# A two-layer image kernel: weights of the final sum on both partition halves, tokens kept by partition, VectorE in the last strips' attention

## The chip, the core and the metric

The kernel runs on one core of a Trainium2 chip. Its engines work side by side, each in the order of its own instruction queue: TensorE (PE) multiplies matrices into PSUM, VectorE (DVE) and ScalarE (ACT) work on SBUF and PSUM, GpSimd (POOL) works on SBUF, and SyncE (SP) issues DMAs. ScalarE issues DMAs too; all of them run on the core's 16 DMA engines. The metric is the device time of one execution in microseconds (us); lower is better.

## What is computed

The input x has 16 images of 64 x 64 pixels and 128 channels, all in f32. First a group norm and a 3x3 convolution give each channel of each pixel an offset, and x is sampled at the moved place by bilinear interpolation. Then comes an attention in which each token attends among the 16 entries of each of its own 8 heads, and at last a mixture of 64 experts, in which each expert takes the 8 tokens of an image that score highest for it.

```python
x = x + deformable_sample(group_norm(x))            # conv gives the offsets
t = to_tokens(x)                                    # 16 images, 4096 tokens, 128 channels
qkv = layer_norm(t) @ w_qkv + b_qkv                 # per head of 16 channels:
attn = softmax((q * C ** -0.5)[..., :, None] * k[..., None, :])
t = t + einsum('bhlij,bhlj->bhli', attn, v) @ w_proj + b_proj

n = layer_norm(t)
probs = softmax(n @ gate_w.T + gate_b, over tokens)
vals, idx = top_k(probs, 8)                         # per image and expert
pooled = sum over the 8 of vals * n[idx]            # one vector per image and expert
h = gelu([pooled, 1] @ weight1[expert])
out_e = [h, 1] @ weight2[expert]                    # 16 images x 64 experts x 128
t[idx] += vals * out_e                              # back to the chosen tokens
```

The kernel writes the last line as a dense sum: for each image a matrix of weights (64 experts x 4096 tokens, zero where a token wasn't chosen) times the experts' outputs (64 x 128), added to t.

## The kernel before

**Two stages.** `Images` works through the 16 images; `finish` then computes all experts and the final sum. Between the two stand a few tensors in device memory: `t2_d`, the tokens after attention (16 x 2 MB), `wt_d`, the weights of the final sum (16 x 1 MB), and `oe_d`, the experts' outputs.

**The image stage.** An image is cut into 8 strips of 512 pixels (`NCH`, `CHW`), a strip into 4 token tiles of 128 (`NA`). `image()` gathers the instructions of all parts of an image in a `Work` list: the convolution of the next strip, the sampling (`sample`), the attention of the strips behind it (`tokens`), the choice of tokens of the image before (`tail`), and the preparation of the next one (`prep`). Each instruction has a slot. `Work.order()` then simulates the engines with estimated durations and sorts the instructions by when they would be ready (80 ns per slot of haste); the hand-made order is emitted as it comes out. [...] Image 0 and image 15 are emitted by themselves; images 1 to 14 are one loop whose body is emitted once. The instructions of the image stage are all recorded by one helper and stand under line 190 in the profile.

**The attention of a strip** (`tokens`) runs through 8 groups, two per token tile, with four heads each (`group(i)`). For each group: `score` (two instructions of 128 x 1024 on GpSimd: q times k, minus the largest value), `expo` (exponential on ScalarE, sum `den` on VectorE), `weigh` (one more on GpSimd into `ev`, sum `att` on VectorE). The score tiles `sc` are two, used in turn; `ev` is one. At the end `second` adds the projection to the tokens `t1` and stores them to `t2_d`, in two DMAs of 64 partitions each: `strip` puts pixel rows and columns where they belong in the image, and partition 2r+h holds half h of the strip's part of image row r. In the last image nothing follows, so the attention of its last strips runs on by itself once the sampling is over.

**The last stage** (`finish`). Experts are taken in fours: `weights` loads them on SP's queue (three buffers), `layers` computes them (PSUM tiles `hps`, `tps`, `yps2`, two buffers each) and stores the outputs to `oe_d` from ScalarE's queue. The inner function `tokens` (line 1350) loads what the final sum needs of an image: `wt`, 64 partitions of 16 KB, and `t2c`, 128 partitions, by two DMAs in pieces of 2 KB. It has four buffers (`cmb`); four images are loaded early, among the experts. `add` (line 1358) loads the image's expert outputs `oe` on ScalarE's queue and then, for each of 8 strips, multiplies four times (a weight tile of 64 experts x 128 tokens is the stationary operand, `oe` of 64 x 128 the moving one) into one PSUM bank (`cops`, two buffers), adds the bank to the tokens on VectorE, and at the end stores the image in two DMAs from ScalarE's queue. An f32 matmul is two instructions on TensorE, so an image has 64.

The order of `finish` is not made by hand: the framework schedules it and places the waits. On ScalarE's queue it comes out as three loads of oe, then six stores, then the next three loads, and so on.

Of the kernel before, what the change touches and what calls it, by code (L numbers as in the profile page):

```python
# [19 lines left out]
P = 128  # L20
B, IMG, C = 16, 64, 128
NPIX = IMG * IMG
NCH = 8
# [39 lines left out]
@with_exitstack  # L63
def conv_attn_moe_kernel(
    ctx: ExitStack,
    tc: tile.TileContext,
    x: bass.AP,
    conv_w: bass.AP,
    conv_b: bass.AP,
    w_qkv: bass.AP,  # L70
    b_qkv: bass.AP,
    w_proj: bass.AP,
    b_proj: bass.AP,
    gate_w: bass.AP,
    gate_b: bass.AP,
    weight1: bass.AP,
    weight2: bass.AP,
    out: bass.AP,
):
    nc = tc.nc  # L80

    dram = ctx.enter_context(tc.tile_pool(name="dram", bufs=1, space=DRAM))
    t2_d = dram.tile([B, NPIX, C], F32, name="t2_d")
    wt_d = dram.tile([B, E, NPIX], F32, name="wt_d")
    oe_d = dram.tile([B, E, C], F32, name="oe_d")

    const = ctx.enter_context(tc.tile_pool(name="const", bufs=1))
    pooled = const.tile([P, E, B], F32, name="pooled")

    with ExitStack() as s:  # L90
        Images(s, tc, x, conv_w, conv_b, w_qkv, b_qkv, w_proj, b_proj, gate_w, gate_b,
               dram, t2_d, wt_d, pooled).run()
    with ExitStack() as s:
        finish(s, tc, weight1, weight2, pooled, t2_d, wt_d, oe_d, out)
# [232 lines left out]
class Images:  # L327
# [583 lines left out]

    def tokens(self, b, k, slot, dense=False):
        plan = Work(self.nc, self.tc)
# [7 lines left out]

        def copy(ap, t, load):
            for h in range(2):
                at, rows = strip(ap)[:, h], t.rearrange("(r h) a c -> r h (a c)", h=2)[:, h]
                nc.sync.dma_start(*((rows, at) if load else (at, rows)))

# [3 lines left out]
        xres, t1 = self.xres[k % 2], self.t1[k % 2]  # L930
        add(-6, lambda: copy(self.x, xres, True))
        add(0, lambda: nc.scalar.activation(
# [60 lines left out]
        def group(i):  # L993
# [3 lines left out]
                ap[:, nh * i : nh * (i + 1)] for ap in (top, den, att)]  # L997

        def score(i):
            sc, (qs, ks, _), (ts, _, _) = group(i)  # L1000
            nc.gpsimd.tensor_tensor(sc, bcast(qs, 3, HD), bcast(ks, 2, HD), ALU.mult)
            nc.gpsimd.tensor_tensor(sc, sc, bcast(ts, 3, HD), ALU.subtract)

# [6 lines left out]
        def weigh(i):  # L1010
            sc, (_, _, vs), (_, _, at) = group(i)
            nc.gpsimd.tensor_tensor(self.ev, sc, bcast(vs, 2, HD), ALU.mult)
            plan.slot += 2
            nc.vector.tensor_reduce(at, self.ev, AX.X, ALU.add)
# [32 lines left out]
        def second():  # L1047
            v = t1.rearrange("p a c -> p (a c)")
            nc.vector.tensor_tensor(v, self.bank, v, ALU.add)
            copy(self.t2_d, t1, False)  # L1050

# [105 lines left out]
    def image(self, b, before, following):  # L1157
# [25 lines left out]
        for k in range(NCH):  # L1183
            work.take(self.tokens(b, k, STEPS * (k + 1) + 6), 0, end, 0)
            if k + 1 < NCH:
                work.take(self.conv(k + 1, STEPS * k), 0, SLOTS, 0)
# [95 lines left out]
def finish(ctx, tc, weight1, weight2, pooled, t2_d, wt_d, oe_d, out):  # L1282
# [8 lines left out]
    hp = ctx.enter_context(tc.tile_pool(name="exph", bufs=2))  # L1291
    lp = ctx.enter_context(tc.tile_pool(name="cmb", bufs=4))
    pp = ctx.enter_context(tc.tile_pool(name="finp", bufs=2, space=PSUM))
    nf, rows = FF // P, 32
    ident = one.tile([P, P], F32, name="ident2")
# [22 lines left out]
    def layers(e0, w1, b1, w2, b2):  # L1318
# [7 lines left out]
        nc.scalar.activation(h, hps, AF.Gelu)  # L1326
        tps = pp.tile([P, nf, P], F32, name="tps")
        for n in range(nf):
            nc.tensor.transpose(tps[:, n, :], h[:, P * n : P * (n + 1)], ident)  # L1329
        hT = hp.tile([P, nf, P], F32, name="hT")  # L1330
        nc.vector.tensor_copy(hT, tps)  # L1331
        yps = pp.tile([P, C], F32, name="yps2")
        nc.tensor.matmul(yps, chosen, b2, start=True, stop=False)
# [13 lines left out]
    def rows_of(t):  # L1347
        return t.rearrange("(r h) q a c -> r h q (a c)", h=2)

    def tokens(b):  # L1350
        wt = lp.tile([E, NPIX], F32, name="wt")
        nc.sync.dma_start(wt, wt_d[b])
        t2 = lp.tile([P, NCH, NA, C], F32, name="t2c")
        for h in range(2):
            nc.sync.dma_start(rows_of(t2)[:, h], strips(t2_d[b])[:, h])
        return wt, t2

    def add(b, wt, t2):
        oe = hp.tile([E, C], F32, name="oe")
        nc.scalar.dma_start(oe, oe_d[b])  # L1360
        for k in range(NCH):
            ops = pp.tile([P, NA, C], F32, name="cops")
            for a in range(NA):
                nc.tensor.matmul(ops[:, a, :], wt[:, CHW * k + a : CHW * (k + 1) : NA], oe,  # L1364
                                 start=True, stop=True)
            nc.vector.tensor_tensor(t2[:, k], t2[:, k], ops, ALU.add)  # L1366
# [40 lines left out]
```

## Time and profile before

| | us |
|---|---|
| median of 3 runs (9387.57 to 9394.68) | 9387.69 |
| the profiled execution | 9384.91 |
| its span in the trace | 9383.1 |
| image stage and choice of tokens, to about | 8880 |
| experts, from the first weight DMA to the last, SP's queue | 8879.8 to 9053.9 |
| final sum, from the first load of oe to the end | 9066.2 to 9383.1 |
| a repeated image (13 distances between 14 stores of weights, 822.2 to 7877.8) | 542.7 |

Busy times over the whole span: PE 8515.6, VectorE 7196.0, ScalarE 6572.7, GpSimd 7619.6 us. The costliest groups that bear on the change are these (count; busy us in all; mean ns of one): `ev<-sc,qkv` on GpSimd 1024; 2429.6; 2373, `sc<-qkv` 1024; 1987.7; 1941, `sc<-sc,top` 1024; 1988.5; 1943, and on VectorE `den<-sc` 1024; 1239.7; 1211 and `att<-ev` 1024; 1235.4; 1206. In the final sum VectorE's `t2c<-t2c,cops` comes 128 times with 687 ns at the median, always within 2 ns of it.

How to read it: a window's busy time tells which engine had no room there; the chain of waits tells what the end waited for; the queues' shares tell how much of the 16 DMA engines' time a stage used. A share over the whole span mixes the stages, so it is read stage by stage below. The program's names stand without their numbers: `t2c` is the token tile of the final sum, and `t` in the image stage is `t1`; `t2_d` shows as `t_d`.

### The profile page before, as it was taken

How to read it: one execution, taken by the hardware profiler on the slowest of the kernel's cores; microseconds unless marked ns; L12 is line 12 of the kernel's file. 1: busy time of each engine (PE TensorE's matmuls, PEld its weight loads, DVE VectorE, ACT ScalarE, POOL GpSimd, SP SyncE). 2: the span in 40 equal slices, each digit the busy share in tenths (PEclk: the TensorE clock that was granted, in tenths of full speed). 3: DMA queues.
4: the chain of work that ended last, by engine and by line, in shares of the span. 5: the costliest groups of instructions: out<-in, count | busy, mean ns of one | idle time of the engine just before them, and what ended most of it. 6: DMA issues, size and time to landing. Idle time of an engine off the chain costs nothing. (4 is left out here: it accounts for less than half of the span.)

```text
span 9383.1 us, 373512 instructions
## 1 busy us (share of the span) xinstructions
PE 8515.6 (91%) x158305; PEld 4589.8 (49%) x159622; DVE 7196.0 (77%) x10154; ACT 6572.7 (70%) x8082; POOL 7619.6 (81%) x5698
## 2 busy tenths in 40 slices
PE   8999999899999989999998999999999999999467
PEld 4545445454544545454454545445454544444247
DVE  4788787878878887887888788888878788788412
ACT  4777777777777777777777777777777777777300
POOL 2898888889888888988888898988889889889500
PEclk9999999999999999999999999999999999999655
DMA  6666666666676666667666666666666676666277
GB/s 161 178 178 175 178 176 181 175 186 177 178 182 174 182 173 185 179 176 183 173 182 172 183 182 177 182 172 183 172 181 182 177 184 172 179 177 174 77 232 239
DMA packets 1327871, 1672.08 MB, mean 178 GB/s; under 512 B 443680, under 2 KB 660512, under 8 KB 1324128
## 3 DMA queue, kind: packets, MB, share of 16 engines
q1 hardware_dynamic: 1305952, 1613.25, 63.7%
q10 hardware_dynamic: 20224, 34.61, 1.0%
q8 instruction: 1262, 20.68, 1.0%
q14 instruction: 433, 3.55, 0.1%
HBM read 1378.16 MB, written 268.96 MB: 176 GB/s over the span
## 5 line engine op out<-in xcount | busy, mean ns | idle before, releaser
L190 DVE SCALAR_TENSOR_TENSOR prod<-chat,yps 128x1024 f32<-128x1024 f32 x2048 | 2472.2, 1210 | 672.0 <-PE yps L190 214.1
L190 ACT ACTIVATE rhat<-yps 128x1024 f32<-128x1024 f32 x2048 | 2079.9, 1021 | 1112.9 <-PE yps L190 412.1
L190 POOL TENSOR_TENSOR ev<-sc,qkv 128x1024 f32<-128x1024 f32 x1024 | 2429.6, 2373 | 278.5 <-ACT sc L190 232.4
L190 PE MATMUL yps<-rhat,xr 32*32 32x176 f32 (+1 forms) x131072 | 2468.7, 275 | 117.9 <-ACT rhat L190 113.2
L190 PE MATMUL cbank<-pad,wconv 128*128 128x512 f32 x4608 | 2530.3, 636 | 38.4 <-DVE far L190 9.5
L190 PEld LDWEIGHTS yps<-rhat,xr 32*32 32x32 f32 x131072 | 1809.3, 104 | 1199.8 <-ACT rhat L190 451.4
L190 POOL TENSOR_TENSOR sc<-qkv 128x1024 f32<-128x1024 f32 x1024 | 1987.7, 1941 | 81.8 <-POOLq L1202 47.5
L190 POOL TENSOR_TENSOR sc<-sc,top 128x1024 f32<-128x1024 f32 x1024 | 1988.5, 1943 | 45.2 <-ACT top L190 36.4
L190 DVE TENSOR_REDUCE den<-sc 128x64 f32<-128x1024 f32 x1024 | 1239.7, 1211 | 256.7 <-ACT sc L190 256.3
L190 DVE TENSOR_REDUCE att<-ev 128x64 f32<-128x1024 f32 x1024 | 1235.4, 1206 | 259.9 <-POOL ev L190 215.9
L190 ACT ACTIVATE sc<-sc 128x1024 f32<-128x1024 f32 x1024 | 1078.8, 1053 | 447.9 <-POOL sc L190 408.8
L190 ACT ACTIVATE chat<-chat,cbi,csc 128x1024 f32<-128x1024 f32 x1024 | 1260.0, 1235 | 36.3 <-DMA chat<-cc_d 35.7
L190 PE MATMUL yps<-parts,sel 128*128 128x512 bf16 x2779 | 950.6, 385 | 291.7 <-DVE prod L190 255.9
L190 ACT ACTIVATE chat<-chat,cbi 128x1024 f32<-128x1024 f32 x1024 | 1162.5, 1143 | 56.1 <-DMA chat<-cc_d 50.8
L190 PE MATMUL acc<-prod,red 128*32 128x512 f32 x8192 | 1116.2, 613 | 85.9 <-issue 5.3
L190 PEld LDWEIGHTS cbank<-pad,wconv 128*128 128x128 f32 x4608 | 741.9, 190 | 902.8 <-issue 769.1
L190 PEld LDWEIGHTS <-sel 128*128 128x128 bf16 x4096 | 355.2, 98 | 1124.5 <-issue 1074.7
L190 DVE RECIPROCAL den<-den 128x128 f32<-128x128 f32 x512 | 479.9, 937 | 4.3
L190 PE MATMUL bank<-wqkv,tr 128*128 128x384 f32 x1024 | 419.5, 505 | 17.5 <-DVE qkv L190 11.1
L190 PEld LDWEIGHTS acc<-prod,red 128*32 128x32 f32 x8192 | 164.2, 108 | 446.3 <-issue 438.0
L190 DVE SCALAR_TENSOR_TENSOR qkv<-bank,rstd,bqkv 128x384 f32<-128x384 f32 x512 | 309.4, 604 | 93.2 <-PE bank L190 92.8
L190 DVE SCALAR_TENSOR_TENSOR cd<-cbank,cb,iot 128x256 f32<-128x256 f32 x512 | 229.1, 474 | 185.4 <-PE cbank L190 185.3
(162 smaller groups left out, 8124.2 us busy)
## 6 DMA issues: line engine op xcount, KB each, us to landing
chat<-cc_d SPq DMA_DIRECT2D x8192, 128.0 KB
xr<-xn_d SPq DMA_DIRECT2D x512, 128.0 KB
pc_d<-pc SPq DMA_DIRECT2D x128, 384.0 KB
parts<-pc_d SPq DMA_DIRECT2D x768, 64.0 KB
xl<-in_x_dram SPq DMA_DIRECT2D x128, 256.0 KB
xres<-in_x_dram SPq DMA_DIRECT2D x256, 128.0 KB
xn_d<-wt SPq DMA_DIRECT2D x128, 256.0 KB
cc_d<-cd SPq DMA_DIRECT2D x128, 256.0 KB
```

What stands on the lines that cost most here:

```text
L190: getattr(engine, fn)(*args, **kwargs)
```

## The change

It has three parts.

1. In the final sum the 4096 columns of weights of an image are put on both halves of the partitions: experts for the first 2048 tokens on partitions 0 to 63, for the last 2048 on 64 to 127, by two DMAs. `oe` is loaded twice, once on each half. Strips k and k + 4 are then multiplied in turn, the one from the lower 64 rows of the array and the other from the upper 64, into two PSUM banks. `cops` gets four banks in a pool of its own; `tps` and `yps2` go down to one bank each. The `cmb` pool has five buffers instead of four, and five images are loaded early, after every third group of experts, instead of four.
2. `t2_d` holds the tokens as they lie in SBUF: per image and partition, all 8 strips one behind the other (16 KB). A strip is stored by one DMA of 128 rows of 2 KB instead of two, and an image is loaded by one DMA with 16 KB per partition instead of two with 2 KB pieces.
3. In the last image, `engine(i)` gives `score` and `weigh` of some groups to VectorE: of strip 6 the groups 4 and 7, of strip 7 the groups 1, 4 and 7. In all other strips `alone` is 8 and no group moves.

```diff
--- before.py
+++ after.py
@@ -80,7 +80,7 @@
     nc = tc.nc
 
     dram = ctx.enter_context(tc.tile_pool(name="dram", bufs=1, space=DRAM))
-    t2_d = dram.tile([B, NPIX, C], F32, name="t2_d")
+    t2_d = dram.tile([B, P, NCH, NA * C], F32, name="t2_d")
     wt_d = dram.tile([B, E, NPIX], F32, name="wt_d")
     oe_d = dram.tile([B, E, C], F32, name="oe_d")
 
@@ -909,7 +909,8 @@
 
 
 
-    def tokens(self, b, k, slot, dense=False):
+
+    def tokens(self, b, k, slot, dense=False, alone=HEADS):
         plan = Work(self.nc, self.tc)
         nc = plan
 
@@ -919,16 +920,16 @@
                 v = v.rearrange("b r w c -> b (r w) c")
             return v.rearrange("b (r q h a) c -> (b q) r h (a c)", r=IMG, q=NCH, h=2)[k]
 
-        def copy(ap, t, load):
+        def load(ap, t):
             for h in range(2):
-                at, rows = strip(ap)[:, h], t.rearrange("(r h) a c -> r h (a c)", h=2)[:, h]
-                nc.sync.dma_start(*((rows, at) if load else (at, rows)))
+                nc.sync.dma_start(
+                    t.rearrange("(r h) a c -> r h (a c)", h=2)[:, h], strip(ap)[:, h])
 
         def add(rel, fn):
             plan.add(slot + rel, fn)
 
         xres, t1 = self.xres[k % 2], self.t1[k % 2]
-        add(-6, lambda: copy(self.x, xres, True))
+        add(-6, lambda: load(self.x, xres))
         add(0, lambda: nc.scalar.activation(
             self.tr[0], self.acc, AF.Identity, bias=0.0 if dense else self.norm[:, 0:1],
             scale=1.0 if dense else self.norm[:, 1:2]))
@@ -996,10 +997,13 @@
             return self.sc[i % 2], [heads(s, a)[:, hs] for s in range(3)], [
                 ap[:, nh * i : nh * (i + 1)] for ap in (top, den, att)]
 
+        def engine(i):
+            return nc.vector if i >= alone and i % 3 == 1 else nc.gpsimd
+
         def score(i):
             sc, (qs, ks, _), (ts, _, _) = group(i)
-            nc.gpsimd.tensor_tensor(sc, bcast(qs, 3, HD), bcast(ks, 2, HD), ALU.mult)
-            nc.gpsimd.tensor_tensor(sc, sc, bcast(ts, 3, HD), ALU.subtract)
+            engine(i).tensor_tensor(sc, bcast(qs, 3, HD), bcast(ks, 2, HD), ALU.mult)
+            engine(i).tensor_tensor(sc, sc, bcast(ts, 3, HD), ALU.subtract)
 
         def expo(i):
             sc, _, (_, ds, _) = group(i)
@@ -1009,7 +1013,7 @@
 
         def weigh(i):
             sc, (_, _, vs), (_, _, at) = group(i)
-            nc.gpsimd.tensor_tensor(self.ev, sc, bcast(vs, 2, HD), ALU.mult)
+            engine(i).tensor_tensor(self.ev, sc, bcast(vs, 2, HD), ALU.mult)
             plan.slot += 2
             nc.vector.tensor_reduce(at, self.ev, AX.X, ALU.add)
 
@@ -1047,7 +1051,9 @@
         def second():
             v = t1.rearrange("p a c -> p (a c)")
             nc.vector.tensor_tensor(v, self.bank, v, ALU.add)
-            copy(self.t2_d, t1, False)
+            nc.sync.dma_start(
+                at_image(self.t2_d, b).rearrange("b p k f -> (b p) k f")[:, k],
+                t1.rearrange("p a c -> p (a c)"))
 
         plan.together(slot + rel + 5.5, proj)
         add(rel + 6, second)
@@ -1181,7 +1187,8 @@
             for t in range(4, 8):
                 work.add(4 * t - 14, lambda: self.load_rows(work, t))
         for k in range(NCH):
-            work.take(self.tokens(b, k, STEPS * (k + 1) + 6), 0, end, 0)
+            alone = HEADS if following or k < 6 else 4 * (7 - k)
+            work.take(self.tokens(b, k, STEPS * (k + 1) + 6, alone=alone), 0, end, 0)
             if k + 1 < NCH:
                 work.take(self.conv(k + 1, STEPS * k), 0, SLOTS, 0)
         work.add(SLOTS - STEPS - 8, lambda: self.reach(work))
@@ -1289,8 +1296,10 @@
     one = ctx.enter_context(tc.tile_pool(name="finc", bufs=1))
     wp = ctx.enter_context(tc.tile_pool(name="expw", bufs=3))
     hp = ctx.enter_context(tc.tile_pool(name="exph", bufs=2))
-    lp = ctx.enter_context(tc.tile_pool(name="cmb", bufs=4))
+    lp = ctx.enter_context(tc.tile_pool(name="cmb", bufs=5))
     pp = ctx.enter_context(tc.tile_pool(name="finp", bufs=2, space=PSUM))
+    p1 = ctx.enter_context(tc.tile_pool(name="finp1", bufs=1, space=PSUM))
+    cpp = ctx.enter_context(tc.tile_pool(name="cmbp", bufs=4, space=PSUM))
     nf, rows = FF // P, 32
     ident = one.tile([P, P], F32, name="ident2")
     make_identity(nc, ident)
@@ -1324,12 +1333,12 @@
                              start=False, stop=True)
         h = hp.tile([P, FF], F32, name="h")
         nc.scalar.activation(h, hps, AF.Gelu)
-        tps = pp.tile([P, nf, P], F32, name="tps")
+        tps = p1.tile([P, nf, P], F32, name="tps")
         for n in range(nf):
             nc.tensor.transpose(tps[:, n, :], h[:, P * n : P * (n + 1)], ident)
         hT = hp.tile([P, nf, P], F32, name="hT")
         nc.vector.tensor_copy(hT, tps)
-        yps = pp.tile([P, C], F32, name="yps2")
+        yps = p1.tile([P, C], F32, name="yps2")
         nc.tensor.matmul(yps, chosen, b2, start=True, stop=False)
         for n in range(nf):
             for e in range(EG):
@@ -1347,23 +1356,31 @@
     def rows_of(t):
         return t.rearrange("(r h) q a c -> r h q (a c)", h=2)
 
+
+
     def tokens(b):
-        wt = lp.tile([E, NPIX], F32, name="wt")
-        nc.sync.dma_start(wt, wt_d[b])
+        wt = lp.tile([P, NPIX // 2], F32, name="wt")
+        for h in range(2):
+            nc.sync.dma_start(wt[E * h : E * (h + 1)], wt_d[b][:, NPIX // 2 * h :][:, : NPIX // 2])
         t2 = lp.tile([P, NCH, NA, C], F32, name="t2c")
+        nc.sync.dma_start(t2.rearrange("p k a c -> p k (a c)"), t2_d[b])
+        return wt, t2
+
+    def add(b, wt, t2):
+        oe = hp.tile([P, C], F32, name="oe")
         for h in range(2):
-            nc.sync.dma_start(rows_of(t2)[:, h], strips(t2_d[b])[:, h])
-        return wt, t2
-
-    def add(b, wt, t2):
-        oe = hp.tile([E, C], F32, name="oe")
-        nc.scalar.dma_start(oe, oe_d[b])
-        for k in range(NCH):
-            ops = pp.tile([P, NA, C], F32, name="cops")
+            nc.scalar.dma_start(oe[E * h : E * (h + 1)], oe_d[b])
+        for k in range(NCH // 2):
+            ops = [cpp.tile([P, NA, C], F32, name="cops") for _ in range(2)]
             for a in range(NA):
-                nc.tensor.matmul(ops[:, a, :], wt[:, CHW * k + a : CHW * (k + 1) : NA], oe,
-                                 start=True, stop=True)
-            nc.vector.tensor_tensor(t2[:, k], t2[:, k], ops, ALU.add)
+                for h in range(2):
+                    es = slice(E * h, E * (h + 1))
+                    nc.tensor.matmul(
+                        ops[h][:, a, :], wt[es, CHW * k + a : CHW * (k + 1) : NA], oe[es],
+                        start=True, stop=True)
+            for h in range(2):
+                at = k + NCH // 2 * h
+                nc.vector.tensor_tensor(t2[:, at], t2[:, at], ops[h], ALU.add)
         for h in range(2):
             nc.scalar.dma_start(
                 strips(out[b].rearrange("r w c -> (r w) c"))[:, h], rows_of(t2)[:, h])
@@ -1371,7 +1388,7 @@
     early = []
     for i, e0 in enumerate(range(0, E, EG)):
         layers(e0, *weights(e0))
-        if i % 4 == 2:
+        if i % 3 == 2:
             early.append(tokens(len(early)))
     for b in range(B):
         add(b, *(early[b] if b < len(early) else tokens(b)))
```

More of the change, by code (lines that the diff above doesn't have):

```diff
@@ L1350, in tokens @@
     def tokens(b):
-        wt = lp.tile([E, NPIX], F32, name="wt")
-        nc.sync.dma_start(wt, wt_d[b])
+        wt = lp.tile([P, NPIX // 2], F32, name="wt")
+        for h in range(2):
+            nc.sync.dma_start(wt[E * h : E * (h + 1)], wt_d[b][:, NPIX // 2 * h :][:, : NPIX // 2])
         t2 = lp.tile([P, NCH, NA, C], F32, name="t2c")
-        for h in range(2):
-            nc.sync.dma_start(rows_of(t2)[:, h], strips(t2_d[b])[:, h])
+        nc.sync.dma_start(t2.rearrange("p k a c -> p k (a c)"), t2_d[b])
         return wt, t2
     def add(b, wt, t2):
-        oe = hp.tile([E, C], F32, name="oe")
-        nc.scalar.dma_start(oe, oe_d[b])
-        for k in range(NCH):
-            ops = pp.tile([P, NA, C], F32, name="cops")
-            for a in range(NA):
-                nc.tensor.matmul(ops[:, a, :], wt[:, CHW * k + a : CHW * (k + 1) : NA], oe,
-                                 start=True, stop=True)
-            nc.vector.tensor_tensor(t2[:, k], t2[:, k], ops, ALU.add)
+        oe = hp.tile([P, C], F32, name="oe")
[3 more added lines that the diff above has]
+            ops = [cpp.tile([P, NA, C], F32, name="cops") for _ in range(2)]
+            for a in range(NA):
+                for h in range(2):
[3 more added lines that the diff above has]
+                        start=True, stop=True)
+            for h in range(2):
+                at = k + NCH // 2 * h
+                nc.vector.tensor_tensor(t2[:, at], t2[:, at], ops[h], ALU.add)
         for h in range(2):
```

## The prediction, written before the result was known

> **What bounds the kernel now.** I first read the busy time by stretch (the columns after the window and its length: PE, weight load, VectorE, ScalarE, GpSimd, each in us, then clock, DMA share, GB/s), because a share over 9383 us hides the stages.
>
> ```profile
> 8500.00:8550.00 50.00, 49.35 (x1007) 24.05 (x1014) 40.47 (x57) 38.40 (x45) 46.88 (x36) 1.00 0.62 173
> 8700.00:8750.00 50.00, 26.57 (x467) 13.54 (x471) 35.24 (x55) 23.26 (x31) 48.84 (x37) 0.76 0.17 49
> 8750.00:8800.00 50.00, 10.34 (x27) 5.55 (x27) 25.44 (x36) 11.97 (x18) 49.32 (x38) 0.53 0.03 11
> 9150.00:9200.00 50.00, 39.43 (x170) 39.16 (x169) 14.35 (x22) 0.00 (x0) 0.00 (x0) 0.50 0.92 295
> 9300.00:9350.00 50.00, 44.62 (x191) 44.66 (x192) 15.85 (x23) 0.00 (x0) 0.00 (x0) 0.50 0.62 202
> ```
>
> Three regimes: the image pipeline, where PE and GpSimd are both full; the last image's end (8700 to about 8815), where GpSimd alone is full and VectorE half idle; and the final sum after 9066, where PE and DMA share the load. The chain of waits (start, us, what) shows how they share it:
>
> ```profile
> 9066.16 1.99 DMA oe<-oe_d
> 9068.18 45.18 PE cops L1364 x192
> 9113.38 0.70 DVE t2c L1366
> ...
> 9115.79 16.50 DMA oe<-oe_d
> 9132.42 45.15 PE cops L1364 x192
> ...
> 9305.38 45.15 PE cops L1364 x192
> 9350.55 0.70 DVE t2c L1366
> 9351.25 7.47 issue
> 9358.72 15.29 PE cops L1364 x64
> ```
>
> Images go in threes: 192 matmuls in 45.15 us (235 ns each, 64 per image, so 15.05 us per image), then PE stands until the next oe has landed behind the stores. These stops are 19.1, 10.6, 13.1, 13.9 and 8.2 us, mean 13.0. So 241 of 317 us are PE and the rest is waiting. The DMA queues of 9066 to 9384 (packets, MB, share of 16 engines):
>
> ```profile
> q1 hardware_dynamic: 13632, 37.75, 40.0%
> q10 hardware_dynamic: 18176, 34.08, 29.8%
> ```
>
> Together 70% of 318 us, 222 us. Stores (q10): 94.8 us for 16 images, 5.9 each. For the loads I cut windows in which one kind is alone on q1: weights wt in 9085 to 9098, then tokens t2c in 9135 to 9147.
>
> ```profile
> q1 hardware_dynamic: 80, 1.05, 36.2%
> q1 hardware_dynamic: 1197, 2.35, 53.1%
> ```
>
> wt: 36.2% of 13 us is 4.7 us for 1.05 MB, 223 GB/s. t2c: 53.1% of 12 us is 6.4 us for 2.35 MB, 369 GB/s, 5.7 us per image of 2.1 MB.
>
> [...]
> - [...] Here no two 64-row tiles run at once; but the 32x32 tiles of yps do: 64 matmuls in 1.23 us in the timeline, with 275 ns for one.
> - [...]
> - [...] in one-element sums that differ only in where an input lies:
>
> ```profile
> L190 DVE TENSOR_TENSOR gmv<-gmv 128x1 f32<-128x1 f32 x32 | 23.4, 731 | 1.1
> L190 DVE SCALAR_TENSOR_TENSOR gmv<-bank,gmv 128x1 f32<-128x1 f32 x16 | 2.4, 152 | 0.5 <-PE bank L190 0.5
> ```
>
> - [...]
>
> **The change part by part**, against the profiled execution: 9384.9 us, span 9383.1 and 1.8 around it. The median of the runs is 2.8 above it.
>
> *PE in the final sum.* 64 matmuls per image stay, but neighbours lie in the two row halves: 32 x 235 ns = 7.5 us per image, 120 in all. Bounds: 15.05 (no overlap) and 7.5; I take 7.5 because of yps. VectorE needs 8 x 0.69 = 5.5 us per image and is not next; the four cops banks let PE fill two while two are drained.
>
> *DMA in the final sum: what is late next.* wt comes in two half DMAs; I take 4.7 us as before[...] (bounds 2.9, its bytes at 369 GB/s, and 4.7). t2c comes as 128 packets of 16 KB in one DMA instead of 1024 of 2 KB in two; nearest row 5.7[...]; I take 5.4. From above: 9.4, if [...] the 16 KB packets, which wt has too, made its 223 GB/s. Stores stay at 5.9. Three images now cost PE 22.5 + 13.0 of stop = 35.5 us and DMA 3 x (4.7 + 5.4 + 5.9) = 48 us; at the best share seen in 50 us, 0.92, that is 52. So DMA sets the pace. 11 images are loaded in the stage (five beforehand instead of four): 11/3 x 52 = 191. The other five stores: 5 x 5.9 / 0.92 = 32. Start: oe 2, PE of one image 7.5, first store's way 2, so 12. End: last sum to last byte, 8 as before (9375 to 9383). Sum 243 against 317: **-74**. Bounds: no gap in the DMA (176 + 29.5 + 20 = 226, -91) and a share of 0.70 as now (206 / 0.70 + 2 = 296, -21). The second oe DMA costs ScalarE's queue about 0.6 us an image, in front of the waiting matmuls; DMA as the pace covers it; without that cover five stops grow by 3 us in all. On SP one DMA more for wt and one fewer for t2c cancel.
>
> *Expert layers (8880 to 9066).* A fifth image is loaded between the weights on SP, before the last ones: 4.7 + 5.4 = 10.1 us of DMA where the share is mostly 0.8 to 0.9, less 4 x 0.3: **+10**. Bounds 0 (it fits the gaps) and +13. One buffer for tps and yps2 costs nothing: the next group's 3.9 us of hps matmuls stand between a tps and its 0.70 us copy; exposed it would be 16 x 1 us.
>
> *Last strips' attention.* A group costs GpSimd 1.93 + 1.93 + 2.34 = 6.2 us. Strip 6 gives away groups 4 and 7, strip 7 groups 1, 4, 7: 31 us off GpSimd. On VectorE no such instruction is in the trace; nearest is prod, equal in shape, 1.21 us: 3.6 per group. [...] 5 x (6.2 - 3.6) = 13 net. VectorE, in order, waits with each of 15 instructions for a GpSimd one of about 2 us; behind it stand the den and att reductions that free sc and ev, which GpSimd needs. VectorE goes from 25 to some 42 busy of 50 us; I give back 3: **-10**. Bounds: -31 [...] and +5 (reductions late). The tail of logits and pooling (8815 to 8880) only shifts.
>
> *Tokens by partition in the loop.* One t2_d store per strip instead of two: SP loses an issue of 0.54 us, 8 per image, same bytes, same 2 KB packets. It isn't on the chain: **0**. But the planner sorts all instructions by simulated readiness, so one sync item fewer can shift the order of everything in 16 images. I take ±16 us (0.2% of 14 x 543 us, the length of a repeated image).
>
> Sum: -74 + 10 - 10 + 0 = -74: 9311 for such an execution, **9314** as a median.
>
> **Rivals.**
> - *Long packets (0.12).* t2c at 9.4 us: three images 60 us, /0.92 = 65; 11/3 x 65 + 32 + 20 = 290, -27; layers +10 + 5 x 3.7 = +28; attention -10: -9, 9379. For: wt is the only load with such packets and the slow one. [...]
> - *No overlap in the array (0.05).* 15.05 us per image stay: 241 + 65 of stops + 3 = 309, -8; with +10 and -10 it is 9380. For: clock 0.50 and weight loads (39.16 of 39.43 us) fill the time; they could be served singly. Against: yps.
> - *A better pack (0.10).* No gaps and wt at 2.9: 226 - 11 x 1.8 = 206, -111; attention -31; layers +5: -137, 9251. For: sums for which 0.92 was reached. [...]
> - *The loop's new order is worse (0.08): slower.* In the 14 repeated images PE and GpSimd are both at 94% or more, SP issues loads in the planner's order, and a product waits where its column is late. It decides from 74 / 14 = 5.3 us (1.0%) per image; at 7.5 us it is +105 - 74 = +31: 9419. Against: the removed issue only unloads SP.
>
> **How the numbers follow.** Forecast 0.65: 9314, own range 9280 to 9350. Faster by over 0.2% (19 us, about what a measurement here can tell from no change) is below 9369: the forecast, the better pack and a third of the long packets (layers' gaps), 0.65 + 0.10 + 0.04 = 0.79, plus 0.05 of the two PE/DMA rivals helped by the loop: 0.84. Same 0.08. Slower 0.08. Range 9272 to 9375: it leaves out 0.08 slower, half of the better pack and a part of the rivals near 9380.
>
> **What would show it.** Right: three images' cops in 22 to 25 us; a DMA share over 0.85 from about 20 us into the sum until the loads end; t2c packets of 16 KB at 5 to 6 us per image; GpSimd's last ev about 10 us earlier; the loop at 543 us per image. Wrong: cops at 15 us per image; DMA idle while PE waits for oe (then order and not bandwidth bounds, and the sum stays near 296); GpSimd no earlier in spite of 15 instructions fewer; a loop length changed by more than 1 us per image.

## The result and the profile after

The changed kernel takes 9292.88 us (median of 4 runs, 9286.93 to 9295.11) against 9389.76 us for the kernel before (4 runs, 9387.57 to 9394.68): a ratio of 0.9895, 95% interval 0.9878 to 0.9912. The profiled execution takes 9292.38 us with a span of 9290.6, 92.5 us less than that of before.

To see where they went I cut both spans at the same marks: the first and the last of the 14 stores of weights in the loop (13 repeated images lie between), SP's first load of expert weights, the issue of the first oe, the end. "Last image" is what lies between the last loop store and the first expert load, "layers" from there to oe. All in us, one profiled execution each; the lower rows belong to the experiments below. The loop of after stands unchanged in e1, e3 and e4 and takes 541.4 to 541.6 us there, so 0.7 us per repeated image, 8 us in all, is within the spread of single executions; the final sum of after stands unchanged in e3, e9 and e12 and takes 245.2 to 246.0.

| kernel | first store | repeated image | last image | layers | final sum | median of runs |
|---|---|---|---|---|---|---|
| before | 822.2 | 542.74 | 1002.0 | 186.4 | 316.9 | 9389.76 |
| after | 817.9 | 542.08 | 986.9 | 192.9 | 245.9 | 9292.88 |
| e1, halves in turn | 815.2 | 541.62 | 989.9 | 192.9 | 322.6 | 9364.25 |
| e2, tokens by image | 823.6 | 542.73 | 991.4 | 198.5 | 231.8 | 9302.33 |
| e3, GpSimd alone | 815.1 | 541.41 | 999.4 | 194.5 | 246.0 | 9304.13 |
| e4, oe at once | 816.1 | 541.64 | 989.1 | 194.2 | 204.0 | 9245.47 |
| e5, wt in one load | 815.4 | 541.6 | 989.8 | 181.5 | 237.5 | 9273.81 |
| e6, e4 and e5 | 815.0 | 541.4 | 988.9 | 182.0 | 187.4 | 9213.45 |
| e7, e2 and e4 | 821.2 | 542.64 | 996.0 | 198.5 | 207.2 | 9278.29 |
| e8, before, oe at once | 823.2 | 542.7 | 1000.4 | 191.6 | 254.5 | 9325.91 |
| e9, two stores, order of after | 814.4 | 542.74 | 989.0 | 193.6 | 245.9 | 9306.64 |
| e10, neighbouring weights | 816.5 | 541.68 | 988.6 | 180.7 | 184.2 | 9213.57 |
| e11, e2, order of after | 819.7 | 543.18 | 989.9 | 196.3 | 232.0 | 9297.53 |
| e12, after, order of e2 | 822.9 | 542.94 | 990.0 | 193.2 | 245.2 | 9309.76 |

The change by stage: image 0 -4.3, the 13 repeated images -8.5, last image -15.1, layers +6.5, final sum -71.0 (each rounded).

The final sum of after, first by busy time in windows (columns as in the prediction; the first window is the end of the first burst and PE's first stop, the second to fourth hold a burst of three images and a stop each, the fifth the last such burst and its stop):

```profile
9060.00:9097.00 37.00, 10.46 (x87) 10.14 (x85) 7.71 (x12) 0.00 (x0) 0.00 (x0) 0.62 0.98 351
9097.00:9147.00 50.00, 23.77 (x195) 23.45 (x197) 15.42 (x24) 0.00 (x0) 0.00 (x0) 0.67 0.92 319
9147.00:9196.00 49.00, 22.89 (x193) 22.56 (x191) 15.42 (x24) 0.00 (x0) 0.00 (x0) 0.67 0.94 325
9196.00:9241.00 45.00, 23.31 (x192) 22.96 (x192) 15.42 (x24) 0.00 (x0) 0.00 (x0) 0.73 0.93 331
9241.00:9273.00 32.00, 22.79 (x192) 22.63 (x192) 15.41 (x24) 0.00 (x0) 0.00 (x0) 0.82 0.55 201
```

Three images now cost PE 23 us instead of 45, and the DMA share is 0.92 to 0.94 over each of the three full bursts with their stops. The chain of waits of after shows what lies between the bursts (start, us, what):

```profile
9046.77 15.52 PE cops L1378 x126
...
9063.62 10.94 DMA out_dram<-t2c
...
9074.64 22.19 DMA oe<-oe_d
...
9096.97 15.18 PE cops L1378 x127
...
9113.49 11.74 DMA out_dram<-t2c
...
9125.30 21.09 DMA oe<-oe_d
```

A load of oe of 32 KB, 2.0 us at the start of the stage, takes 20 to 22 us behind the stores (22.19, 21.09, 21.64 and 19.73 between the bursts). At the first three stops the first such load isn't even issued when PE stops: the chain shows it going out 0.1 us after a store of 11 to 12 us has landed, about 4 us into the stop. PE's stops are 26.1, 25.9, 25.4, 22.2 and 8.7 us in the timeline. The last one, in front of the last image, was 8.2 before; the mean of the other four went from 14.2 to 24.9. So a burst lost 22 us and each of four stops gained 10.7. While a burst runs, DMA isn't full: this shorter window of after covers most of the second one.

```profile
9097.00:9112.00 15.00, 15.00 (x129) 15.00 (x129) 8.99 (x14) 0.00 (x0) 0.00 (x0) 0.81 0.78 230
```

The queues of after over 9044.7 to 9290.6 (packets, MB, share of 16 engines), which answer to the two of before:

```profile
q1 hardware_dynamic: 3344, 34.61, 40.6%
q10 hardware_dynamic: 19456, 34.61, 39.5%
```

Loads: 40.6% of 245.9 us over 11 images is 9.1 us each. Stores: 6.1 us for each of 16.

The last image's attention in after, by windows, and then VectorE's share of it by tile (count; min/median/max ns):

```profile
8700.00:8750.00 50.00, 21.39 (x188) 11.02 (x189) 44.90 (x62) 16.75 (x24) 46.38 (x36) 0.64 0.03 11
8750.00:8800.00 50.00, 13.21 (x33) 6.76 (x34) 33.61 (x38) 11.77 (x20) 31.70 (x26) 0.53 0.04 16
```

```profile
L190 DVE TENSOR_TENSOR sc<-qkv x5: 1216/1802/2096, 8715.3 to 8775.8; 128x1024 f32<-128x1024 f32 x5
L190 DVE TENSOR_TENSOR sc<-sc,top x5: 1208/1677/2523, 8717.2 to 8778.8; 128x1024 f32<-128x1024 f32 x5
L190 DVE TENSOR_TENSOR ev<-sc,qkv x5: 1194/1216/2908, 8720.8 to 8783.6; 128x1024 f32<-128x1024 f32 x5
```

VectorE is now busy 44.9 of 50 us where it had 35.2, and GpSimd ends earlier. Most of VectorE's instructions above wait for GpSimd's, and GpSimd's for them. An example of each, GpSimd's timeline and then VectorE's (start, us, what):

```profile
8727.77 1.93 POOL L190 TENSOR_TENSOR sc<-sc,top 128x1024 f32<-128x1024 f32 x1
8729.66 1.44 POOL L190 TENSOR_TENSOR att<-att,den 128x128 f32<-128x128 f32 x1
```

```profile
8728.68 2.10 DVE L190 TENSOR_TENSOR sc<-qkv 128x1024 f32<-128x1024 f32 x1
```

Twelve of the fifteen start while an instruction of GpSimd runs, and each of them ends 1.1 us after that one, whether it started 0.1 or 1.8 us before its end; the shortest of the fifteen takes 1.19 us and the longest 2.91. The four of GpSimd's `att<-att,den` that start under one of VectorE's take 1.43 to 1.44 us, against 0.46 at the median of all 512.

### The profile page after: what moved, and what is told of

The parts are those of the page before. It is cut to its first block, busy times and chain, and to the rows that moved or that the text cites. A ratio compares the mean times of both kernels' runs of the same rounds, so it can differ in the third digit from the quotient of the medians.

```text
span 9290.6 us, 373103 instructions
## 1 busy us (share of the span) xinstructions
PE 8406.4 (90%) x158230; PEld 4481.1 (48%) x159622; DVE 7213.4 (78%) x10169; ACT 6574.0 (71%) x8082; POOL 7600.8 (82%) x5683
## 5 line engine op out<-in xcount | busy, mean ns | idle before, releaser
L190 PE MATMUL yps<-rhat,xr 32*32 32x176 f32 (+1 forms) x131072 | 2497.6, 275 | 109.5 <-ACT rhat L190 104.6
```

The lines of the kernel that those rows point to most:

```text
L190: getattr(engine, fn)(*args, **kwargs)
```

## The experiments

Each kernel is after with the edit shown, unless it says otherwise. Ratios are to before.

**e1: do the two halves overlap?** The same matmuls on the same halves, but all of the lower half first, so that no two neighbours lie in different row groups.

```diff
-        for k in range(NCH // 2):
-            ops = [cpp.tile([P, NA, C], F32, name="cops") for _ in range(2)]
-            for a in range(NA):
-                for h in range(2):
-                    es = slice(E * h, E * (h + 1))
+        for h in range(2):
+            for k in range(NCH // 2):
+                ops = cpp.tile([P, NA, C], F32, name="cops")
+                es = slice(E * h, E * (h + 1))
+                for a in range(NA):
...
```

> The changed kernel, but all four strips of the lower partition half are multiplied before the four of the upper half, so that neighbouring matmuls share a row half again; all loads, stores and layouts stay. Stage lengths of the changed kernel: final sum 245.9 us (first oe load to the end), its cops 124 us of PE time. My theory (overlap of the two row halves is what halved PE's part, and DMA then took over): about 15 us per image on PE again, three images 45 us plus a stop of 13 to 20; the final sum 295 to 320 us, the whole 50 to 70 us over the changed kernel (9340 to 9360). Rival (the token layout and the fifth early image made the gain, PE was never the pace): final sum within 15 us of 246, 9293 to 9308.

Measured: 9364.25 us, ratio 0.9974 (0.9963 to 0.9984); final sum 322.6 us, 76.7 more than after. PE's timeline in e1:

```profile
9104.83 41.32 PE L1378 MATMUL cops<-oe,wt 64*128 64x128 f32 x192 [22.34 <-DMA oe<-oe_d]
9168.66 41.32 PE L1378 MATMUL cops<-oe,wt 64*128 64x128 f32 x192 [22.51 <-DMA oe<-oe_d]
```

That is 215 ns for each matmul, near the 235 of before, and three of the four stops for oe between the bursts are over 22 us all the same (the fourth is 14.7). Taking turns between the row halves is what takes PE's time from 41.3 to 23 us; layout, five buffers and long packets together gain nothing in this stage without it. What the fifth buffer and the fifth early image are worth by themselves no run shows.

The granted clock differs too: 0.50 throughout these bursts of e1, up to 1.00 in those of after. It isn't the cause. In after's second burst the clock rises from 0.50 to 1.00, and 2 us hold 21 matmuls (those that reach into the window counted) on either side:

```profile
9099.00:9101.00 2.00, 2.00 (x21) 2.00 (x20) 1.28 (x2) 0.00 (x0) 0.00 (x0) 0.50 0.98 418
9107.00:9109.00 2.00, 2.00 (x21) 2.00 (x20) 1.42 (x3) 0.00 (x0) 0.00 (x0) 1.00 1.09 248
```

**e2: what is the layout of the tokens worth?** `t2_d` and its stores and loads as in before.

```diff
-    t2_d = dram.tile([B, P, NCH, NA * C], F32, name="t2_d")
+    t2_d = dram.tile([B, NPIX, C], F32, name="t2_d")
...
-        nc.sync.dma_start(t2.rearrange("p k a c -> p k (a c)"), t2_d[b])
+        for h in range(2):
+            nc.sync.dma_start(rows_of(t2)[:, h], strips(t2_d[b])[:, h])
```

> The changed kernel with the tokens laid out by image rows as before: two stores per strip, two loads of 2 KB pieces per image. My theory: loads of an image cost 0.3 us of DMA time more or nothing, so the final sum grows by 11 x 0.3 / 0.92, 4 us, to about 250; the order of the image stage returns to that of before, so the repeated image goes from 542.1 back to 542.7 us and the first weight DMA comes 10 to 13 us later: 9305 to 9312 in all. Rival (the 16 KB packets are what speeds the final sum): final sum 275 us or more, 9325 or more.

Measured: 9302.33 us, 0.9906 (0.989 to 0.9923). Both theories missed: the final sum is 14 us shorter than in after, at 231.8. Its queues over 9069 to 9300.8, and then the loads of oe between its bursts, from its chain of waits:

```profile
q1 hardware_dynamic: 13376, 34.61, 47.3%
q10 hardware_dynamic: 19456, 34.61, 41.0%
```

```profile
9102.71 12.41 DMA oe<-oe_d
...
9142.66 16.51 DMA oe<-oe_d
...
9184.80 19.97 DMA oe<-oe_d
...
9231.35 20.34 DMA oe<-oe_d
```

An image's loads take more DMA time here (47.3% of 231.8 over 11 is 10.0 us against 9.1), and yet oe arrives sooner at the first two of these stops; the later two take nearly as long as in after. PE's four stops are 19.5, 19.3, 22.4 and 23.8 us, 14.5 less in sum. The loads' 34.61 MB are 13376 packets here and 3344 in after. One reading is that a 16 KB packet of a load holds up the stores and oe on the other queue for longer than one of 2 KB does; how the DMA engines choose between two queues no run shows. The trace fits this reading in part (the first two stops); e7 tests what follows from it.

**e3: what does VectorE's help bring?** `alone = HEADS` for every strip.

```diff
-            alone = HEADS if following or k < 6 else 4 * (7 - k)
+            alone = HEADS
```

> The changed kernel, but GpSimd does all groups of the last strips' attention. The loop and the final sum are as in the changed kernel. My theory ([...] each group given away nets 6.2 - 3.6 us): first weight DMA 10 to 16 us later than 8852, the whole 9303 to 9309. Rival (no exclusion, 31 us): 9320 or more. Second rival (VectorE's waits eat it): within 5 us of 9293.

Measured: 9304.13 us, 0.991 (0.9893 to 0.9926); last image 999.4 us against 986.9. So the five groups gain 12.5 us in this pair of executions, not the 31 that they take off GpSimd. Over all kernels the last image takes 986.9 to 991.4 us with VectorE's help (996.0 in e7) and 999.4 to 1002.0 without, so the gain lies between 8 and 15 us. In e3's windows GpSimd is the full one again, and VectorE has room:

```profile
8700.00:8750.00 50.00, 12.67 (x42) 7.14 (x41) 27.93 (x47) 10.63 (x16) 49.52 (x39) 0.54 0.01 5
```

**e4: does DMA or the order set the pace of the sum?** All outputs of the experts come in by two DMAs ahead of the sum, so that no load of oe stands behind stores. The bytes are the same.

```diff
-        oe = hp.tile([P, C], F32, name="oe")
-        for h in range(2):
-            nc.scalar.dma_start(oe[E * h : E * (h + 1)], oe_d[b])
...
+    oe = one.tile([P, B, C], F32, name="oe")
+    for h in range(2):
+        nc.scalar.dma_start(oe[E * h : E * (h + 1)], oe_d.rearrange("b e c -> e b c"))
```

> The changed kernel, but the experts' outputs for all images are loaded once, by two DMAs ahead of the final sum, so no image waits for its oe behind the stores. In the changed kernel PE waits 22 to 26 us for oe between threes while the DMA share is 0.92 to 0.98. My theory (bandwidth is the pace and the wait for oe only shows it): PE waits for wt or t2c instead, the middle of the stage keeps its pace of 16 to 16.5 us per image, and only the end (9241 to 9290, share 0.55 and 0.33) shortens: final sum 225 to 240, the whole 9275 to 9288. Rival (the order, oe behind stores, is the pace): the stops vanish, final sum below 215, 9262 or less.

Measured: 9245.47 us, 0.9847 (0.9831 to 0.9864); final sum 204.0 us. The rival won. PE's timeline in e4, two pieces, and a window of its middle:

```profile
9047.00 50.86 PE L1375 MATMUL cops<-oe,wt 64*128 64x128 f32 x416 [9.61 <-DMA oe<-oe_d]
9102.35 8.33 PE L1375 MATMUL cops<-oe,wt 64*128 64x128 f32 x64 [4.49 <-DVE t2c L1380]
```

```profile
9100.00:9200.00 100.00, 58.29 (x448) 56.91 (x448) 35.33 (x56) 0.00 (x0) 0.00 (x0) 0.69 1.03 369
```

PE works off what is loaded (416 matmuls, six and a half images) without a stop, and then goes at the pace at which images arrive: 9102.35 to 9224.90 is nine images at 13.6 us, where after needed 49.6 / 3 = 16.5. The share is 1.03 over 100 us and the rate 369 GB/s, so 0.92 at 319 was no ceiling. (A mean busy share can't exceed 1, so the count runs a little high; the bytes of the rate don't depend on it.)

**e5: does a load in two halves cost something?** `wt_d` is stored as two halves, so that one DMA fills all 128 partitions.

```diff
...
-        for h in range(2):
-            nc.sync.dma_start(wt[E * h : E * (h + 1)], wt_d[b][:, NPIX // 2 * h :][:, : NPIX // 2])
+        nc.sync.dma_start(wt, wt_d[b].rearrange("h e n -> (h e) n"))
```

> The changed kernel, but wt_d is laid out by halves (2 x 64 experts x 2048 tokens), so that the weights of an image come in one DMA over all 128 partitions instead of one per half. Loads of oe stay behind the stores. [...] q1's time per image (40.6% of 245.9 us for 11 images, 9.1 us) falls by up to 1.8 us, the stops for oe shorten by as much per image, final sum 246 to 228 to 238. Rival (the two halves overlap with other traffic, nothing is lost): final sum within 4 us of 246.

Measured: 9273.81 us, 0.9876 (0.986 to 0.9893); layers 181.5 instead of 192.9, final sum 237.5 instead of 245.9. The loads' queue was busy for 38.8% of the 237.5 us, 8.4 us per image against 9.1: 0.7 us less, where up to 1.8 was said. So the load in two halves costs time as it stands; why, no run shows. The edit also saves a DMA per image and puts each half in one piece in device memory; what these two are worth was not parted from it.

**e6: both.** The edits of e4 and e5 together.

> Both: oe loaded once for all images, and wt in one DMA over 128 partitions. With oe at once the final sum was 204 us with the DMA engines busy throughout (48.5 + 45.7% over it, more than 1.0 in every 20 us from 9060 to 9220). [...] 11 x 1.8 = 20 us less, final sum 182 to 190, the whole 9222 to 9235. Rival [...]: final sum 200 to 206, 9240 to 9250.

Measured: 9213.45 us, 0.9812 (0.9796 to 0.9829), the best of all kernels here; final sum 187.4. Its queues over the sum, and a window of 130 us:

```profile
q10 hardware_dynamic: 18976, 34.61, 49.6%
q1 hardware_dynamic: 3168, 34.60, 44.8%
```

```profile
9060.00:9190.00 130.00, 92.62 (x755) 91.48 (x753) 58.65 (x92) 0.00 (x0) 0.00 (x0) 0.79 1.03 416
```

With 416 GB/s over 130 us and PE busy for 71% of them, this is the case that the prediction described: DMA sets the pace. e10 below bears it out: there PE is faster and the time stays.

**e7: are the short pieces better, or only fairer to oe?** e2's layout with e4's single load.

> oe loaded once, and the tokens laid out by image rows as before the change. With tokens by image alone the final sum was 231.8 us, 14 shorter than in the changed kernel, though its loads took more DMA time (47.3% of 231.8 us against 40.6% of 245.9). Theory: [...] a 16 KB load packet delays the 2 KB stores and the oe behind them; without oe behind stores the advantage of small pieces goes, and the final sum is 204 to 218. Rival (the layout by partition is slower in itself): 188 to 197.

Measured: 9278.29 us, 0.988 (0.9863 to 0.9896); final sum 207.2 against e4's 204.0. Short pieces gain 14 us when oe stands behind the stores and lose 3 when it doesn't. That fits the reading that long packets hold up what stands on the other queue; no run shows how the engines divide their time between the two.

**e8: the old array use with the new order.** Before, with oe loaded once. To make room the expert weights have two buffers instead of three, so the layers differ a little too (191.6 against 186.4).

```diff
-    wp = ctx.enter_context(tc.tile_pool(name="expw", bufs=3))
+    wp = ctx.enter_context(tc.tile_pool(name="expw", bufs=2))
...
+    oe = one.tile([E, B, C], F32, name="oe")
+    nc.scalar.dma_start(oe, oe_d.rearrange("b e c -> e b c"))
```

> The kernel before, with oe loaded once ahead of the final sum and, for room, two buffers of expert weights instead of three (the expert layers may take longer for it; the final sum is read by itself). PE has 16 x 15.05 = 241 us there. If PE was the pace and the 13.0 us stops for oe were the rest: the stops go, final sum 250 to 262 us against 317. Rival (DMA was the pace in the kernel before too, 222 us at 0.92 [...]): 275 or more.

Measured: 9325.91 us, 0.993 (0.9914 to 0.9947); final sum 254.5. PE's timeline in e8 is one line:

```profile
9076.25 239.91 PE L1362 MATMUL cops<-oe,wt 64*128 64x128 f32 x1024 [8.76 <-DMA oe<-oe_d]
```

One DMA in the place of 16 takes 62 us off the old sum, against 71 for the change in this stage.

**e9, e11, e12: why is the repeated image 0.7 us shorter in after?** Two causes were open: one store issue less on SP for each strip, or the order, since the planner sorts one instruction fewer. e9 keeps the layout and the planned order of after and issues a strip's store in two DMAs.

```diff
...
+            def store():
+                for h in range(2):
+                    nc.sync.dma_start(to[:, h], rows[:, h])
+
+            plan.together(plan.slot, store)
```

> The changed kernel in its own planned order of the image stage, but each strip's token store is issued as two DMAs of 64 rows into the same layout (the planner sees them as one item). The repeated image takes 541.4 to 542.1 us in the kernels with one store and 542.6 to 542.7 in those with two stores in the image layout. If the gain comes from the other order that the planner finds for one item fewer: it stays at 541.4 to 542.1. Rival (the saved issue of 0.54 us on SP, eight per image): back to 542.4 or more. The final sum stays at 246 us either way.

Measured: 9306.64 us, 0.9912 (0.9895 to 0.9928); 542.74 us per repeated image, as before, which seemed to speak for SP's issues. But SP's waits in e9, over 543 us, have a line that neither before nor after has:

```profile
SPq L190 <- DMA t_d<-t: 22.4, 8, 4.5
```

Issued back to back, the second store waits for the first to land; before, other work lay between the two. Who asks for this wait, the chip or the framework that places semaphores, no run shows. So e9 parts nothing. e11 tried the same with e2's layout, in which I thought the two wouldn't meet.

> The tokens by image in t2_d as in e2 (two stores of 64 rows a strip, loads in 2 KB pieces), but the two stores recorded as one item, so that the planned order is that of after. In e9 the second store waited on SP for the first to land (22.4 us an image), which kept SP longer than the old pair did; here the two don't touch one another and shouldn't wait. Two stores take SP about 1.07 us against 0.37, so 8 x 0.7 = 5.6 us of SP an image. Theory A (the order makes the loop's gain): the repeated image stays at 541.4 to 542.1 us. Theory B (SP's issue time makes it): it goes back to 542.5 or more. Either way the final sum takes what e2's took, 228 to 236 us. Image 0, to the first store of weights: 814 to 818 us in both, since it went with the order in all runs so far (821 to 824 in the old one).

Measured: 9297.53 us, 0.9899 (0.9883 to 0.9916); the wait is there again, 20.9 us an image, and a repeated image takes 543.18 (image 0, said 814 to 818, 819.7). The final sum of 232.0 repeats e2's. e12 turns it around: the planner is shown two stores and orders as in e2, and one DMA is issued.

```diff
...
+            for h in range(2):
+                nc.sync.dma_start(to[:, h], t1.rearrange("(r h) a c -> r h (a c)", h=2)[:, h])
+            plan.ops[-2].emits = []
+            plan.ops[-1].emits = [("dma_start", (
                 at_image(self.t2_d, b).rearrange("b p k f -> (b p) k f")[:, k],
+                t1.rearrange("p a c -> p (a c)")), {})]
```

> After with the planned order of e2 (which has two store items a strip, as before): the planner is shown two stores of 64 rows, and one DMA of 128 rows is issued in the place of the second. So SP issues as little as in after, in the old order; t2_d and all else are as in after. e11 and e9 could not part the two, since there the second store waited on SP for the first to land. Theory A (the order makes the loop's gain): the repeated image takes 542.5 to 542.8 us and the first weights are stored at 821 to 824 us. Theory B (SP's issues make it): 541.4 to 542.1 us. Final sum 244 to 248 us in both, as in after.

Measured: 9309.76 us, 0.9917 (0.9901 to 0.9934). The loop's stores of weights in e12 and then in after (first and last start):

```profile
L190 SPq MOVE wt_d<-big x14: 29/29/38, 822.9 to 7881.1; - x14
```

```profile
L190 SPq MOVE wt_d<-big x14: 29/29/29, 817.9 to 7865.0; - x14
```

13 distances of 542.94 us with SP's issues as few as in after, and image 0 at 822.9: both as in the old order. So one issue less brings nothing without the new order. Over all kernels, the seven in the new order with one store a strip take 541.4 to 542.1 us per repeated image and the five in the old order 542.6 to 542.9; the groups lie apart, though the 0.6 us between them is no more than the spread within the first. Whether the new order would keep its gain with a second store that doesn't wait stays open, since in e9 and e11 it did wait.

**e10: what sets PE's pace now?** e6 with 128 neighbouring columns of `wt` as weights instead of every fourth one. Tokens then get the weights of other tokens, so the output differs; the work is the same in size.

```diff
-                        ops[h][:, a, :], wt[es, CHW * k + a : CHW * (k + 1) : NA], oe[es, b],
+                        ops[h][:, a, :], wt[es, CHW * k + P * a :][:, :P], oe[es, b],
```

> The kernel with oe at once and wt in one load, but the weight tiles of the final sum are read as 128 neighbouring columns instead of every fourth; the weights then meet other tokens, so the sum's output is another. Read is PE's pace over the first five images, where nothing is waited for: 120 to 122 ns per matmul instruction with every fourth column, with the granted clock at 1.00 as at 0.66. If the reading of every fourth column paces the weight loads: 60 to 100 ns. Rival (a weight load of 128 f32 columns takes that long by itself): 110 to 122 ns. The length of the final sum stays near 187 us, since DMA is its pace.

Measured: 9213.57 us, a single execution; final sum 184.2. The weight loads in e6 and then in e10 (min/median/max ns), and PE's timeline of each after the start:

```profile
L1375 PEld LDWEIGHTS cops<-oe,wt x1024: 304/326/328, 9030.0 to 9196.9; 64*128 64x128 f32 x171
```

```profile
L1375 PEld LDWEIGHTS cops<-oe,wt x1024: 182/188/335, 9033.2 to 9196.1; 64*128 64x128 f32 x171
```

```profile
9029.97 58.59 PE L1375 MATMUL cops<-oe,wt 64*128 64x128 f32 x480 [9.21 <-DMA oe<-oe_d]
```

```profile
9035.53 27.94 PE L1375 MATMUL cops<-oe,wt 64*128 64x128 f32 x344 [0.24 <-DMA oe<-oe_d]
```

122 ns per matmul with every fourth column, 81 with neighbours. So the strided read of the weights paces PE in e6. In e10 the next limit shows at once, VectorE, which has to take the banks out:

```profile
9046.00:9056.00 10.00, 9.73 (x140) 8.20 (x138) 10.00 (x18) 0.00 (x0) 0.00 (x0) 1.00 1.03 386
```

VectorE is busy for all of these 10 us, and 344 matmuls are 43 banks of 0.68 us, 29 us, about what PE takes for them. So 81 ns is VectorE's pace and not that of the weight loads alone. The time of the kernel doesn't move, since DMA is the bound in both.

## Why the prediction was right, and where it wasn't

The forecast was 9314 us and the median is 9292.88, inside both ranges and 21 us below the number. By its terms:

*Final sum: said -74, is -71.0.* The number is right, one step under it isn't.
- "I take 7.5" us of PE per image: right. 124.4 us of PE in the stage, 7.8 per image, and three images in 23 us. e1 shows that the overlap does it: 41.3 us without, and not by the clock, which stood at 0.50 in a part of after's burst as well. Rival "no overlap" is out.
- "t2c 5.4, wt 4.7": together 10.1, is 9.1. The 5.4 was the author's estimate, a little under the 5.7 measured before; the 4.7 was carried over from the load of before, and that two half loads cost as much was an estimate too. Rival "long packets" is out as it was priced, a slow t2c. The long packets do have a cost while oe stands behind the stores, 14 us (e2), which is gone with oe loaded ahead (e7); that it comes from what they hold up fits, but isn't shown.
- "At the best share seen in 50 us, 0.92, that is 52. So DMA sets the pace": this step failed. Three images took 49.6 us at a share of 0.92 to 0.94, which looks like a confirmation, but with the same bytes e4 ran at 1.03 and 13.6 us per image, and e6 at 416 GB/s. What sets the pace in after is a cycle in two parts that don't cover each other: a burst in which DMA has too little to do (0.78), since, as I read it, the stores come out only as PE finishes, and a stop in which DMA works off stores and loads ahead of the next oe. The prediction priced the old stop at 13.0 us and let it vanish under the DMA. The four stops for oe grew to 24.9 in the mean instead. The error of leaving the cycle out met the error of taking 0.92 for a limit, and that the two come to the right number is luck. Loading oe ahead takes 42 us more off the stage (e4), and 58 us together with e5's load (e6).
- The prediction's own sign for this, DMA idle while PE waits for oe, was the wrong sign: the first window above, most of it the first stop, has a share of 0.98. It falls to 0.78 in the first 15 us of the second burst, while PE works.

*Expert layers: said +10, is +6.5*, for the fifth image's loads. e5 shows that the two-DMA load of `wt` is more than all of it: 11.4 us for five images, with which the stage would be shorter than before.

*Last strips' attention: said -10, is -12.5 by e3* (-15.1 for the stretch between the two profiles). The size fits the estimate: 31 us leave GpSimd, and if it stands while VectorE's instructions run (3.6 us for each of five groups), 13 of them are left. That it stands was not shown by the kernel before: the two one-element lines in the prediction (731 and 152 ns) differ in operation too. After shows it: VectorE's instructions end 1.1 us after GpSimd's, and GpSimd's `att<-att,den` takes 1.43 us for 0.46. Not all 15 wait, as was said, but 12, for 0.1 to 1.8 us. GpSimd's last `ev` starts 912.9 us after the last loop store instead of 933.4, but what ends last is now group 7 on VectorE, so not all of these 20 us arrive at the end.

*Loop: said 0 ± 16, is -12.8 with image 0.* The reasoning holds in both its halves: an issue less on SP is worth nothing in the old order (e12), and the planner's new order brought something that couldn't be told ahead. That this order is better by 0.7 us per image and 4 to 5 in image 0 is luck of the sort, and the 0.7 us is about the spread of single executions; rival "the loop's new order is worse" had the right mechanism with the other sign. Why the one order is shorter stays open.

The sum of the terms, -74, misses -92.5 by 18.5 (rounded): loop -12.8, attention and the rest of that stretch -5.1, layers -3.5, final sum +3.0. The largest part is the term that was left at zero for want of a sign.

Rival "a better pack" asked for gaps closed and `wt` at 2.9 us and gave 206 us for the sum. The change doesn't do that; e4 reaches 204 and e6 187. A slip in the working of the rival "Long packets": the layers' extra is 5 x 4.0 us against the 5.4 taken elsewhere, not 5 x 3.7, which moves that rival by under 2 us.

## What to carry to other kernels

When an engine in a chain is made twice as fast, don't carry its old waits over (four stops of PE went from 14.2 to 24.9 us in the mean here), and don't take a busy share near one for the bound (0.92 at 319 GB/s in after, but 369 GB/s in e4 and 416 in e6): ask what stands in front of the late transfer on its own queue. A small load that everything waits for should not stand behind stores that wait for the work that follows from the last such load (2.0 us for oe at the start of the stage, 20 to 22 behind stores); one DMA for all of them, ahead of the stage, was worth nearly as much on the old kernel as the whole change in that stage (62 us against 71). And when instructions are sorted by a planner, an edit that adds or removes one can reshuffle the rest, so an effect of some tenths of a per cent in a loop needs a run that keeps the order fixed.

## What was unexpected of the hardware

- A weight load of 64 x 128 in f32 took 326 ns when it read every fourth column and 188 ns with neighbouring ones, and the pace of matmuls went from 122 to 81 ns, where VectorE had become the limit. The 326 ns are the same where the granted clock is 0.50 (e1, whose matmuls run one after the other without a gap) and where it is 1.00 (e6).
- Two stores of 64 partitions each to one tensor, issued back to back on SP, took 3.4 to 4 us of its queue instead of about 1.1, since the second was held until the first had landed (e9, e11); by whom stays open.
- A 32 KB load between bursts took 20 to 22 us behind stores when the other queue moved `t2c` in packets of 16 KB, and 12 to 20 us when it moved it in packets of 2 KB (after, e2).
